# Selective scan with partition = (state, channel of a group of 8), and first-layer attention with maxima

## The chip, the core and the metric

The kernel runs on one core of one Trainium2 chip. The core has a matrix engine (TensorE, PE), a vector engine (VectorE, DVE), an activation engine (ScalarE, ACT), a general engine (GpSimd, POOL) and SyncE (SP), which here only starts transfers. Each works through its own queue in order and waits on semaphores for the others. SBUF is the working memory of 128 partitions, PSUM the small memory that TensorE writes. The metric is the device time of one execution in microseconds (us); before the change it is 20378.7 us, the median of three runs from 20369.83 to 20399.26.

## The reference

The input is 8 images of 64 channels, 64 x 64 pixels (L = 4096 positions), in fp32. Four layers follow each other:

- Layer 0: attention of every position to every position, then a depthwise 3x3 convolution, a 1x1 convolution and a residual.
- Layer 1: a patch norm, then two blocks of 8x8-window attention with 8 heads, each with an MLP.
- Layer 2: a 3x3 filter whose taps depend on position and channel, then a 1x9 convolution.
- Layer 3: a selective scan in four directions over 128 channels with 16 states, then gated output and a multi-scale modulation.

What the change touches is this:

```
# layer 0
scores = einsum('bdn,bdm->bnm', Q, Q) / c ** 0.5        # Q = x, 64 x 4096 per image
prob = softmax(scores, axis=-1)
out = einsum('bnm,bdm->bdn', prob, V)                   # V = relu(bn(w1 x))

# layer 3, for each image, direction k, channel d and state n
h = h * exp(dt_t * A) + dt_t * B_t * u_t                # over 4096 positions t
y_t = sum over n of h * C_t
```

## The kernel before, in words

All is fp32. `tile_kernel` goes through the images in four pairs; the two images of a pair share the 128 partitions, 64 channels each, except in layer 3's scan, which takes one image at a time with its 128 inner channels on the partitions. The whole kernel is unrolled. A scheduler orders each engine's queue from the program and gives out buffers: a pool hands a tile of a tag to the next user when its last user is done, so the number of buffers of a tag sets how far engines run ahead of each other. Five large slabs (one holds 128 x 4356 values) serve X, the padded attention output, values and so on.

**Attention of layer 0** (`layer0_direct`). Both images are worked at once. For each of four column pieces of 1024 and each of 32 row tiles, TensorE makes scores `sd` for image 0 (partitions 0 to 63) and image 1 (64 to 127), each a matmul of 64 rows, so the two use different halves of the array. ScalarE takes the exponential without subtracting a maximum and adds up its rows (`ed`, L508). Then `weigh` (L484) multiplies by the values, one image into PSUM partitions 0 to 63, the other into 64 to 127. At the end the result is multiplied by the reciprocal sums (`prd`). The sums are kept, and at the end of the program `in_range` tests them and a branch would repeat everything with `layer0`, which subtracts maxima; in the runs shown it isn't taken. `block0` is the convolution behind the attention.

**Scan of layer 3** (`ss2d`, `scan_inputs`, `scan`). A unit is a direction `k` and a piece of TC = 1024 positions; an image has 16 units. `scan_inputs` makes B, C (rows `xd`, written to DRAM as `rows`) and the step dt and `dtu` = dt x u, each 128 channels on the partitions. `scan` then loops over the 16 states `n`: SyncE loads B_n and C_n broadcast to all partitions (`bc`, 1 MB, L974), ScalarE makes the decay `da` = exp(dt A_n) (L976), VectorE multiplies dtu by B_n (L978), runs the recurrence (L981) and multiplies by C_n (L985), and TensorE adds the 16 states in PSUM through an identity (`collect`, L969). ScalarE copies the last column as the carry for the next piece (L984). After half the states the next unit's inputs are made (`ahead`).

Lines that the prediction uses beside these: L855 and L860 (`pi`, `pz`: the projection into layer 3, 64 rows), L919 and L935 (`px`, `pd`: B and C, and dt, in `scan_inputs`), L810 and L822 (`pb`, `py`: taps and 1x9 convolution in layer 2), L633 (`kx`: keys times a head mask, on GpSimd, in the window attention), L645 (its scores plus bias, from PSUM), L815 (adding a tap), L319 (squares in a norm, from PSUM), L466 and L471 (`pvd`, values of the attention).

Of the kernel before, what the change touches and what calls it, by code (L numbers as in the profile page):

```python
# [24 lines left out]
TC = 1024  # L25
# [52 lines left out]
def _pack(w):  # L78
# [17 lines left out]
    put("w1T", _dup(f["w1"][:, :, 0, 0].T))  # L96
# [94 lines left out]
class _Net:  # L191
# [39 lines left out]
    def prepare(self):  # L231
# [10 lines left out]
        nc.vector.tensor_tensor(self.w1a[0:64, :], w["w1T"][0:64], sc[0:64, 0, :], ALU.mult)  # L242
        nc.vector.tensor_copy(self.w1a[64:65, :], sc[64:65, 1, :])

        self.w1bd = const.tile([P, P], F32, name="w1bd", tag="w1bd")
        nc.gpsimd.memset(self.w1bd, 0.0)
        for im in range(2):
            lo = slice(64 * im, 64 * im + 64)
            nc.vector.tensor_tensor(self.w1bd[lo, lo], w["w1T"][lo], sc[lo, 0, :], ALU.mult)
        self.b1row = const.tile([1, 8, C], F32, name="b1row", tag="b1row")  # L250
        nc.vector.tensor_copy(self.b1row, sc[0:1, 1, :].unsqueeze(1).to_broadcast([1, 8, C]))
        self.ones = const.tile([P, P], F32, name="ones", tag="ones")
        nc.gpsimd.memset(self.ones, 1.0)
        self.sums = const.tile([P, B // 2, 2, 32], F32, name="sums", tag="sums")
# [30 lines left out]
        self.A = const.tile([P, KDIR, NST], F32, name="A", tag="A")  # L285
        nc.scalar.activation(self.A, w["alog"], AF.Exp)
        nc.vector.tensor_scalar(self.A, self.A, -1.0, None, ALU.mult)
# [51 lines left out]
    def layer0(self, p):  # L339
# [6 lines left out]
        with ExitStack() as st:  # L346
# [78 lines left out]

            self.block0(X, pad, wk, ps, "m")
        return X

    def block0(self, X, pad, wk, ps, tag):

        nc, w = self.nc, self.w
        if True:
            cv = self.flat("cv")
            self.dwconv(cv.rearrange("p (h w) -> p h w", w=64), pad, w["dw2"], None, 64)
            for c in range(NCH):
# [4 lines left out]
                pw = ps.tile([P, CH], F32, name="pw", tag=tag)  # L440
# [4 lines left out]

    def layer0_direct(self, p):

        nc, tc, w = self.nc, self.tc, self.w
        X = self.flat("X")
        nc.sync.dma_start(X, self.x[2 * p : 2 * p + 2].rearrange("b c h w -> (b c) (h w)"))
        pad = self.slab("att").rearrange("p (h w) -> p h w", w=66)
        self.pad_border(pad, 66)
        VT = self.flat("VT").rearrange("p (t c) -> p t c", c=P)
        NB = 1024
        with ExitStack() as st:
            wk = st.enter_context(tc.tile_pool(name="w0d", bufs=2))
            ps = st.enter_context(tc.tile_pool(name="ps0d", bufs=3, space=PSUM))  # L460
            pso = st.enter_context(tc.tile_pool(name="ps0o", bufs=1, space=PSUM))

            for g in range(4):
                pv = ps.tile([P, 8, P], F32, name="pvd", tag="s")
                for h in range(2):
                    nc.tensor.matmul(  # L466
                        pv[:, 4 * h : 4 * h + 4, :], lhsT=self.ones[0:1, :], rhs=self.b1row, start=True, stop=False
                    )
                    for j in range(4 * h, 4 * h + 4):
                        t = 8 * g + j  # L470
                        nc.tensor.matmul(  # L471
                            pv[:, j, :], lhsT=X[:, t * P : (t + 1) * P], rhs=self.w1bd, start=False, stop=(j % 4 == 3)
                        )
                nc.scalar.activation(VT[:, 8 * g : 8 * g + 8, :], pv, AF.Relu)

            parts = wk.tile([P, 2, 32, 4], F32, name="parts", tag="parts", bufs=1)
            half = (slice(0, 64), slice(64, 128))
            for jc in range(L // NB):
                po = pso.tile([P, NB], F32, name="pod", tag="po")

                def weigh(t, es):
                    for h in range(2):
                        for im in range(2):
                            nc.tensor.matmul(  # L484
                                po[half[im], h * CH : (h + 1) * CH],
                                lhsT=VT[:, t, half[im]],
                                rhs=es[im][:, h * CH : (h + 1) * CH],
                                start=(t == 0),
                                stop=(t == 31),
                            )  # L490

                last = None
                for t in range(32):
                    ss = [ps.tile([P, NB], F32, name=f"sd{im}", tag="s") for im in range(2)]
                    for h in range(2):
                        o = jc * NB + h * CH
                        for im in range(2):
                            nc.tensor.matmul(  # L498
                                ss[im][:, h * CH : (h + 1) * CH],
                                lhsT=X[half[im], t * P : (t + 1) * P],  # L500
# [450 lines left out]
    def scan(self, XC, Y, unit, ready, ahead, pools):  # L951
# [20 lines left out]
        for n in range(NST):  # L972
# [14 lines left out]
            if n == NST // 2:  # L987
                following = ahead()
# [107 lines left out]
```

## Time and profile before

| what | value |
|---|---|
| median of three runs | 20378.7 us |
| profiled execution: time / span | 20399.26 us / 20397.1 us |
| instructions in the profile | 109912 |
| busy: PE / DVE / ACT / POOL | 68% / 73% / 31% / 3% |
| mean granted TensorE clock | 0.756 of full |
| one pair of images | 5.1 ms, of which attention 0.53 ms and two scans 1.42 ms each |
| HBM read | 2159.55 MB |

The span is the time from the first to the last instruction. A matmul of 512 fp32 columns appears as two records. "PEclk" is the share of its clock that the throttle granted TensorE: 1.00 or 0.50 at any instant, so a value between is a mixture. In a line of groups stand line, engine, operation, tiles, shape and count, then busy us, mean ns of one, the idle time of the engine before them, and what ended it. The form "64*128 64x512" of a matmul means 64 rows of the array by 128 columns in use, and a moving operand of 64 partitions by 512.

### The profile page before, as it was taken

How to read it: one execution, taken by the hardware profiler on the slowest of the kernel's cores; microseconds unless marked ns; L12 is line 12 of the kernel's file. 1: busy time of each engine (PE TensorE's matmuls, PEld its weight loads, DVE VectorE, ACT ScalarE, POOL GpSimd, SP SyncE). 2: the span in 40 equal slices, each digit the busy share in tenths (PEclk: the TensorE clock that was granted, in tenths of full speed). 3: DMA queues.
4: the chain of work that ended last, by engine and by line, in shares of the span. 5: the costliest groups of instructions: out<-in, count | busy, mean ns of one | idle time of the engine just before them, and what ended most of it. 6: DMA issues, size and time to landing. Idle time of an engine off the chain costs nothing.

```text
span 20397.1 us, 109912 instructions
## 1 busy us (share of the span) xinstructions
PE 13968.1 (68%) x37466; PEld 4708.2 (23%) x37466; DVE 14790.1 (73%) x12346; ACT 6242.7 (31%) x9357; POOL 611.1 (3%) x803
## 2 busy tenths in 40 slices
PE   9787565565978765556597876655659787565665
PEld 3332111111333211111133321111113332111111
DVE  0555998998065599899806559989980656998998
ACT  5331322332533133233253313323325331322332
POOL 0110000000011000000001100000000110000000
PEclk9776776777977677787697767777779776766776
DMA  0000554553000055455300005545530000554553
GB/s 12 1 1 17 196 192 140 197 193 133 4 1 1 21 196 192 143 197 191 130 3 1 1 24 195 192 141 196 192 129 2 1 1 28 195 192 142 197 191 122
DMA packets 569244, 2191.99 MB, mean 107 GB/s; under 512 B 35424, under 2 KB 35424, under 8 KB 568032
## 3 DMA queue, kind: packets, MB, share of 16 engines
q1 hardware_dynamic: 562240, 2164.39, 30.8%
q10 hardware_dynamic: 6432, 20.47, 0.4%
q8 instruction: 298, 4.88, 0.1%
q14 instruction: 274, 2.24, 0.0%
HBM read 2159.55 MB, written 25.17 MB: 107 GB/s over the span
## 4 chain that ended last, share of the span: by engine, by line
DVE 39%; PE 33%; DMA 21%; ACT 4%; issue 2%; DVEq 0%; ACTq 0%; POOL 0%
DMA bc<-rows 21%; DVE h L981 14%; DVE v L978 7%; DVE v L985 7%; PE sd L498 5%; PE pod L484 5%; PE ws L642 4%; DVE n_sd L324 4%; PE av L678 2%; PE n_v L321 2%; PE pb L810 2%; PE pt L670 2%; PE py L822 2%; PE wpv L656 1%; DVE XC L310 1%
## 5 line engine op out<-in xcount | busy, mean ns | idle before, releaser
L969 PE MATMUL y<-v,pack 128*128 128x512 f32 x8192 | 6070.3, 883 | 4309.6 <-DVE v L985 4309.6
L969 PEld LDWEIGHTS y<-v,pack 128*128 128x128 f32 x8192 | 1918.4, 258 | 8488.0 <-DVE v L985 6545.5
L981 DVE TENSOR_TENSOR_SCAN h<-da,carry,v 128x1024 f32<-128x1024 f32 x1536 | 3610.4, 2350 | 142.3 <-DVE v L978 1.4
L976 ACT ACTIVATE da<-dt,A 128x1024 f32<-128x1024 f32 x2048 | 2327.8, 1137 | 1896.1 <-DVE h L981 1894.6
L978 DVE TENSOR_TENSOR v<-dtu,bc 128x1024 f32<-128x1024 f32 x2048 | 2505.5, 1223 | 468.6 <-DMA bc<-rows 448.8
L985 DVE TENSOR_TENSOR v<-h,bc 128x1024 f32<-128x1024 f32 x2048 | 2507.4, 1224 | 61.8
L984 ACT ACTIVATE carry<-h 128x1 f32<-128x1 f32 x1536 | 311.5, 203 | 5571.7 <-DVE h L981 5571.6
L324 DVE RECIPROCAL n_sd<-n_sd 128x512 f32<-128x512 f32 x288 | 963.7, 3349 | 594.4 <-ACT n_sd L323 594.3
L508 ACT ACTIVATE ed<-sd 128x1024 f32<-128x1024 f32 x1024 | 1039.2, 1020 | 866.7 <-PE sd L498 866.5
L981 DVE TENSOR_TENSOR_SCAN h<-da,v 128x1024 f32<-128x1024 f32 x512 | 1173.4, 2292 | 45.7 <-DVE v L978 0.5
L517 DVE COPY att<-pod 128x1024 f32<-128x1024 f32 x16 | 19.6, 1226 | 1578.1 <-PE pod L484 1578.1
L642 PE MATMUL ws<-kx,Q 64*64 64x512 f32 x2048 | 1093.8, 727 | 8.5 <-DVE we L645 6.1
L498 PE MATMUL sd<-X 64*128 64x512 f32 x4096 | 1038.5, 617 | 7.7 <-ACT ed L508 7.7
L484 PE MATMUL pod<-ed,VT 128*64 128x512 f32 x4096 | 998.0, 605 | 0.0
L321 PE MATMUL n_v<-n_sq,pack 128*128 128x512 f32 x576 | 513.2, 988 | 424.0 <-DVE H L332 252.9
L919 PE MATMUL px<-XC,pack 128*36 128x512 f32 x512 | 428.7, 978 | 537.8 <-ACT XC L865 332.3
L633 POOL TENSOR_TENSOR kx<-K,pack 128x512 f32<-128x512 f32 x512 | 536.5, 1052 | 4811.0 <-DVE K L624 2902.9
L678 PE MATMUL av<-wv,et 128*64 128x16 f32 x8192 | 508.4, 221 | 143.6 <-ACT et L672 143.6
L678 PEld LDWEIGHTS av<-wv,et 128*64 128x64 f32 x8192 | 457.5, 150 | 442.3 <-ACT et L672 354.4
L498 PEld LDWEIGHTS sd<-X 64*128 64x128 f32 x4096 | 361.2, 187 | 674.4 <-issue 653.4
L319 ACT ACTIVATE n_sq<-n_c 128x512 f32<-128x512 f32 x288 | 171.9, 597 | 1010.4 <-PE n_c L317 1010.3
L691 ACT ACTIVATE oc<-wot,pack 64x128 f32<-64x128 f32 x512 | 185.7, 363 | 908.9 <-PE wot L687 908.9
(216 smaller groups left out, 12958.1 us busy)
## 6 DMA issues: line engine op xcount, KB each, us to landing
bc<-rows SPq DMA_DIRECT2D x2048, 1024.0 KB, 5.2
rows<-xd ACTq DMA_DIRECT2D x128, 128.0 KB, 2.0
X<-in_x SPq DMA_DIRECT2D x4, 2048.0 KB, 7.9
out<-Y SPq DMA_DIRECT2D x32, 256.0 KB, 2.0
pack<-in_w ACTq DMA_DIRECT2D x1, 3169.0 KB, 16.1
pack<-in_w ACTq DMA_DIRECT2D x1, 424.5 KB, 9.2
```

What stands on the lines that cost most here:

```text
L321: nc.tensor.matmul(pv, lhsT=avg, rhs=sq, start=True, stop=True)
L324: nc.vector.reciprocal(sd, sd)
L484: nc.tensor.matmul(po[half[im], h * CH : (h + 1) * CH], lhsT=VT[:, t, half[im]], rhs=es[im][:, h * CH : (h + 1) * CH], start=(t == 0), sto ...
L498: nc.tensor.matmul(ss[im][:, h * CH : (h + 1) * CH], lhsT=X[half[im], t * P : (t + 1) * P], rhs=X[half[im], o : o + CH], start=True, stop= ...
L508: nc.scalar.activation(e, ss[im], AF.Exp, scale=C**-0.5, accum_out=parts[:, im, t, jc : jc + 1])
L642: nc.tensor.matmul(s[lo], lhsT=Q[lo, cols], rhs=kx[lo], start=True, stop=True)
L678: nc.tensor.matmul(av[lo, hd], lhsT=et[:, j, lo], rhs=v[:, im, hd], start=True, stop=True)
L969: nc.tensor.matmul(y[:, hc], lhsT=w["ident"], rhs=v[:, hc], start=(n == 0), stop=(n == NST - 1))
L976: nc.scalar.activation(da, dt, AF.Exp, scale=self.A[:, k, n : n + 1])
L978: nc.vector.tensor_tensor(v, dtu, bc[:, 0, :], ALU.mult)
L981: nc.vector.tensor_tensor_scan(along(h), along(da), along(v), first, ALU.mult, ALU.add)
L985: nc.vector.tensor_tensor(v, h, bc[:, 1, :], ALU.mult)
```

## The change

Two things change at once.

First, the attention of layer 0 goes back to `layer0`, image by image. For each image TensorE makes all scores once for the row maxima (256 matmuls of 64 rows, `s`, VectorE reduces 1024 at a time), the negative maxima are turned into an extra row of the moving operand, and in a second pass scores of 65 rows are made again (`s`, 256 matmuls), exponentiated, and multiplied by the values (`po`, 256 matmuls of 128 rows: the upper half of the columns holds ones and gives the sums). `layer0_direct`, `in_range` and the branch at the end go.

Second, the scan is laid out anew. A unit is now 512 positions (32 units an image). The partitions of a step are 16 states x 8 channels, and the 16 steps `u` of a unit go over the 16 groups of 8 channels. dt x A is made by TensorE into PSUM (`da`, a matmul whose contraction is one strip of 32 channels, `asel`), ScalarE takes the exponential in place in PSUM. `rows` now holds dtu, and SyncE broadcasts it to the 16 states (`ub`, 1 MB for four steps); B and C are made by TensorE with repeated weights (`BB`, `CC`; C a second time in PSUM as `pc`). GpSimd makes dtu x B for all steps and h x C for the even ones, VectorE makes h x C for the odd ones with C from PSUM, and TensorE sums over states with a selecting matrix into one strip of 32 output partitions (`ysel`, `y`). `v` has four buffers, `h` and `da` three, `y` two.

The diff, cut to its core:

```diff
-TC = 1024
+GD = P // NST
+TC = 512
...
-    put("xpT", np.concatenate([xp[:, RNK:], xp[:, :RNK]], axis=1).transpose(2, 0, 1))
-    dtT = f["dtproj_w"].transpose(2, 0, 1)
-    put("dtT", np.concatenate([np.zeros((2 * NST,) + dtT.shape[1:], np.float32), dtT], axis=0))
+    put("xbT", np.repeat(xp[:, RNK : RNK + NST], GD, axis=1).transpose(2, 0, 1))
+    put("xcT", np.repeat(xp[:, RNK + NST :], GD, axis=1).transpose(2, 0, 1))
+    put("xr", xp[:, :RNK].transpose(1, 0, 2))
+    put("dtT", f["dtproj_w"].transpose(2, 0, 1))
+    e32 = np.eye(32, dtype=np.float32)
+    put("gsel", np.concatenate([e32] * 4, axis=0).reshape(P, 4, GD))
+    put("ysel", np.concatenate([e32.reshape(4, GD, 32)] * NST, axis=1).transpose(1, 0, 2))
     put("dtb", f["dtproj_b"].T)
     put("alog", f["A_logs"].reshape(KDIR, DI, NST).transpose(1, 0, 2))
     put("ds", f["Ds"].reshape(KDIR, DI).T)
...
+        self.asel = const.tile([P, KDIR, 4, NST * GD], F32, name="asel", tag="asel")
+        for k in range(KDIR):
+            for q in range(4):
+                nc.vector.tensor_tensor(
+                    self.asel[:, k, q].rearrange("p (n d) -> p n d", d=GD),
+                    A[:, k, :].unsqueeze(2).to_broadcast([P, NST, GD]),
+                    w["gsel"][:, q, :].unsqueeze(1).to_broadcast([P, NST, GD]),
+                    ALU.mult,
+                )
+        self.xdt = const.tile([P, KDIR, P], F32, name="xdt", tag="xdt")
+        with self.tc.tile_pool(name="psw", bufs=1, space=PSUM) as ps:
+            pw = ps.tile([P, KDIR, P], F32, name="pxdt", tag="pxdt")
+            for k in range(KDIR):
+                nc.tensor.matmul(pw[:, k, :], lhsT=w["xr"][:, k, :], rhs=w["dtT"][:, k, :], start=True, stop=True)
+            nc.scalar.activation(self.xdt, pw, AF.Copy)
         self.dsum = const.tile([P, 1], F32, name="dsum", tag="dsum")
...
-    def layer0_direct(self, p):
...
-    def in_range(self):
...
-        nbc = 2 * NST
-        px = ps.tile([P, TC], F32, name="px", tag="pr")
-        for h in range(TC // CH):
-            nc.tensor.matmul(
-                px[0 : nbc + RNK, h * CH : (h + 1) * CH],
-                lhsT=w["xpT"][:, k, :],
-                rhs=xc[:, h * nr : (h + 1) * nr, :],
-                start=True,
-                stop=True,
-            )
-        xd = wk.tile([nbc + RNK, TC], F32, name="xd", tag="xd", bufs=1)
-        nc.scalar.activation(xd, px[0 : nbc + RNK], AF.Copy)
-        rows = self.dram.tile([nbc, TC], F32, name="rows", tag="rows")
-        nc.scalar.dma_start(rows, xd[0:nbc, :])
-        pd = ps.tile([P, TC], F32, name="pd", tag="pr")
+        BB = wk.tile([P, TC], F32, name="BB", tag="BB")
+        CC = wk.tile([P, TC], F32, name="CC", tag="CC")
+        dt = wk.tile([P, TC], F32, name="dt", tag="dt")
+        dtu = wk.tile([P, TC], F32, name="dtu", tag="dtu")
+        db = w["dtb"][:, k : k + 1]
         for h in range(TC // CH):
             hc = slice(h * CH, (h + 1) * CH)
-            nc.tensor.matmul(
-                pd[:, hc], lhsT=w["dtT"][nbc:, k, :], rhs=xd[nbc:, hc], start=True, stop=True
-            )
-        db = w["dtb"][:, k : k + 1]
-        dtu = wk.tile([P, TC], F32, name="dtu", tag="dtu")
-        nc.scalar.activation(dtu, pd, AF.Abs, bias=db)
-        dt = wk.tile([P, TC], F32, name="dt", tag="dt")
-        nc.vector.tensor_scalar(dt, pd, db, 0.0, ALU.add, ALU.max)
+            pd = ps.tile([P, CH], F32, name="pd", tag="pr", bufs=2)
+            nc.tensor.matmul(pd, lhsT=self.xdt[:, k, :], rhs=xc[:, h * nr : (h + 1) * nr, :], start=True, stop=True)
+            nc.scalar.activation(dtu[:, hc], pd, AF.Abs, bias=db)
+            nc.vector.tensor_scalar(dt[:, hc], pd, db, 0.0, ALU.add, ALU.max)
         nc.scalar.activation(dtu, dtu, AF.Exp, scale=-1.0)
         nc.scalar.activation(dtu, dtu, AF.Ln, bias=1.0)
         nc.vector.tensor_tensor(dt, dt, dtu, ALU.add)
         nc.vector.tensor_tensor(
             dtu.rearrange("p (a b) -> p a b", b=64), dt.rearrange("p (a b) -> p a b", b=64), xc, ALU.mult
         )
-        return rows, dt, dtu
+        rows = self.dram.tile([32, 4, TC], F32, name="rows", tag="rows")
+        nc.scalar.dma_start(rows.rearrange("m r t -> r m t"), dtu)
+        for to, wt in ((BB, "xbT"), (CC, "xcT")):
+            for h in range(TC // CH):
+                pb = ps.tile([P, CH], F32, name="pb3", tag="pr", bufs=2)
+                nc.tensor.matmul(pb, lhsT=w[wt][:, k, :], rhs=xc[:, h * nr : (h + 1) * nr, :], start=True, stop=True)
+                nc.scalar.activation(to[:, h * CH : (h + 1) * CH], pb, AF.Copy)
+        return rows, dt, BB, CC
 
     def scan(self, XC, Y, unit, ready, ahead, pools):
 
         nc, w = self.nc, self.w
         wk, ps = pools
         k, c, at = unit
-        rows, dt, dtu = ready
+        rows, dt, BB, CC = ready
         rev = k >= 2
 
         def along(t):
@@ -961,30 +846,53 @@
 
         if at == 0:
             self.carry = wk.tile([P, NST], F32, name="carry", tag="carry")
-        y = ps.tile([P, TC], F32, name="y", tag="y")
-        def collect(n, v):
+        y = ps.tile([P, TC], F32, name="y", tag="y", bufs=2)
+        pc = ps.tile([P, TC], F32, name="pc3", tag="pc", bufs=1)
+        xc = self.piece(XC, k, c)
+        nr = CH // 64
+        for h in range(TC // CH):
+            nc.tensor.matmul(
+                pc[:, h * CH : (h + 1) * CH],
+                lhsT=w["xcT"][:, k, :],
+                rhs=xc[:, h * nr : (h + 1) * nr, :],
+                start=True,
+                stop=True,
+            )
+        following = None
+        for u in range(NST):
+            q, r = u // 4, u % 4
+            g = 4 * r + q
+            rs = slice(32 * r, 32 * r + 32)
+            if r == 0:
+                ubs = wk.tile([P, 4, TC], F32, name="ub", tag="ub")
+                nc.sync.dma_start(
+                    ubs.rearrange("p r t -> p (r t)"),
+                    rows[GD * q : GD * q + GD].rearrange("d r t -> d (r t)").unsqueeze(0).to_broadcast([NST, GD, 4 * TC]),
+                )
+            ub = ubs[:, r, :]
+            da = ps.tile([P, TC], F32, name="da", tag="da", bufs=3)
             for h in range(TC // CH):
                 hc = slice(h * CH, (h + 1) * CH)
-                nc.tensor.matmul(y[:, hc], lhsT=w["ident"], rhs=v[:, hc], start=(n == 0), stop=(n == NST - 1))
-        following = None
-        for n in range(NST):
-            bc = wk.tile([P, 2, TC], F32, name="bc", tag="bc")
-            nc.sync.dma_start(bc, rows[n :: NST, :].unsqueeze(0).to_broadcast([P, 2, TC]))
-            da = wk.tile([P, TC], F32, name="da", tag="da")
-            nc.scalar.activation(da, dt, AF.Exp, scale=self.A[:, k, n : n + 1])
-            v = wk.tile([P, TC], F32, name="v", tag="v")
-            nc.vector.tensor_tensor(v, dtu, bc[:, 0, :], ALU.mult)
-            h = wk.tile([P, TC], F32, name="h", tag="h")
-            first = 0.0 if at == 0 else self.carry[:, n : n + 1]
-            nc.vector.tensor_tensor_scan(along(h), along(da), along(v), first, ALU.mult, ALU.add)
+                nc.tensor.matmul(da[:, hc], lhsT=self.asel[rs, k, q, :], rhs=dt[rs, hc], start=True, stop=True)
+            nc.scalar.activation(da, da, AF.Exp)
+            v = wk.tile([P, TC], F32, name="v", tag="v", bufs=4)
+            nc.gpsimd.tensor_tensor(v, ub, BB, ALU.mult)
+            h3 = wk.tile([P, TC], F32, name="h", tag="h", bufs=3)
+            first = 0.0 if at == 0 else self.carry[:, g : g + 1]
+            nc.vector.tensor_tensor_scan(along(h3), along(da), along(v), first, ALU.mult, ALU.add)
             if at < NTC - 1:
-                end = h[:, 0:1] if rev else h[:, TC - 1 : TC]
-                nc.scalar.activation(self.carry[:, n : n + 1], end, AF.Copy)
-            nc.vector.tensor_tensor(v, h, bc[:, 1, :], ALU.mult)
-            collect(n, v)
-            if n == NST // 2:
+                end = h3[:, 0:1] if rev else h3[:, TC - 1 : TC]
+                nc.scalar.activation(self.carry[:, g : g + 1], end, AF.Copy)
+            if u % 2:
+                nc.vector.tensor_tensor(v, h3, pc, ALU.mult)
+            else:
+                nc.gpsimd.tensor_tensor(v, h3, CC, ALU.mult)
+            for h in range(TC // CH):
+                hc = slice(h * CH, (h + 1) * CH)
+                nc.tensor.matmul(y[rs, hc], lhsT=w["ysel"][:, q, :], rhs=v[:, hc], start=(q == 0), stop=(q == 3))
+            if u == NST // 2:
                 following = ahead()
 
         yp = y.rearrange("p (a b) -> p a b", b=64)
...
 def tile_kernel(ctx: ExitStack, tc: tile.TileContext, x: bass.AP, packs, layout, out: bass.AP):
     net = _Net(ctx, tc, x, packs, layout, out)
     for p in range(B // 2):
-        t = net.layer0_direct(p)
+        t = net.layer0(p)
         t = net.layer1(t)
         t = net.layer2(t)
         net.layer3(t, p)
-    with tc.If(net.in_range() > 0):
-        for p in range(B // 2):
-            t = net.layer0(p)
-            t = net.layer1(t)
-            t = net.layer2(t)
-            net.layer3(t, p)
 
 
 def kernel(**inputs):
```

The attention that returns, in its inner loops (it stood in the file before and is unchanged):

```
for t in range(32):
    for q in range(4):
        s = ps_s.tile([P, 2, CH], F32, name="s", tag="s")
        for h in range(2):
            o = q * 1024 + h * CH
            nc.tensor.matmul(s[:, h, :], lhsT=X[lo, t * P : (t + 1) * P], rhs=X[lo, o : o + CH], start=True, stop=True)
        nc.vector.tensor_reduce(mx[:, t, q : q + 1], s, AX.XY, ALU.max)
```

More of the change, by code (lines that the diff above doesn't have):

```diff
@@ L241, in prepare @@
         self.w1a = const.tile([65, C], F32, name="w1a", tag="w1a")
-        nc.vector.tensor_tensor(self.w1a[0:64, :], w["w1T"][0:64], sc[0:64, 0, :], ALU.mult)
+        nc.vector.tensor_tensor(self.w1a[0:64, :], w["w1T"], sc[0:64, 0, :], ALU.mult)
         nc.vector.tensor_copy(self.w1a[64:65, :], sc[64:65, 1, :])
[L245 to L254, printed above, removed]
         bn = w["bn23"]
```

115 lines of the change are left out of this document (5 added, 110 removed).

## The prediction

> **What bounds the kernel now.** I read the page's engine shares and its 40 slices first. The four image pairs repeat, VectorE (DVE) fills most slices, and TensorE (PE) alone fills the first slice of each pair.
>
> ```profile
> PE 13968.1 (68%) x37466; PEld 4708.2 (23%) x37466; DVE 14790.1 (73%) x12346; ACT 6242.7 (31%) x9357; POOL 611.1 (3%) x803
> ...
> PE   9787565565978765556597876655659787565665
> ...
> DVE  0555998998065599899806559989980656998998
> ...
> PEclk9776776777977677787697767777779776766776
> ```
>
> Next, the engine table of five stretches of the first pair: attention, the nine taps of layer 2, the input projection of layer 3, and one image's scan.
>
> ```profile
> 50.00:180.00 130.00, 129.25 (x535) 41.98 (x536) 1.23 (x1) 71.02 (x133) 0.00 (x0) 1.00 0.00 1
> 1657.00:1687.60 30.60, 29.93 (x34) 6.61 (x32) 16.72 (x22) 3.70 (x6) 0.00 (x0) 0.50 0.00 0
> ...
> 1917.20:1941.00 23.80, 23.80 (x29) 9.32 (x28) 5.17 (x8) 6.09 (x8) 0.00 (x0) 0.50 0.00 0
> 1983.70:3403.00 1419.30, 846.48 (x1153) 259.06 (x1153) 1301.38 (x832) 422.91 (x545) 0.53 (x4) 0.74 0.55 191
> ```
>
> Columns after the window: its length, then PE, PEld, DVE, ACT, POOL busy, the granted clock, DMA. Attention is PE-bound at clock 1.00. The scan is DVE-bound: 1301 of 1419 us. The two middle rows matter most: PE busy without a gap, yet clock 0.50. The timeline of PE shows which matmuls these are:
>
> ```profile
> 1918.09 1.91 PE L855 MATMUL pi<-H,pack 64*128 64x512 f32 x2
> 1919.79 1.91 PE L860 MATMUL pz<-H,pack 64*128 64x512 f32 x2
> 1921.50 1.91 PE L855 MATMUL pi<-H,pack 64*128 64x512 f32 x2
> ...
> 1992.23 3.63 PE L919 MATMUL px<-XC,pack 128*36 128x512 f32 x4
> 1996.96 1.98 PE L935 MATMUL pd<-xd,pack 4*128 4x512 f32 x4 [1.11 <-ACT xd L927]
> ```
> ```profile
> 305.63 1.99 PE L498 MATMUL sd<-X 64*128 64x512 f32 x8
> 307.55 1.94 PE L484 MATMUL pod<-ed,VT 128*64 128x512 f32 x8
> 309.42 1.13 PE L498 MATMUL sd<-X 64*128 64x512 f32 x4
> ```
>
> A matmul of 512 columns is two records. One with 64 rows starts every 1.707 us for 27 us on end and never gets the full clock; 18-row taps (second stretch) neither. px has all 128 rows and only 36 columns, and after it pd runs four records in 1.98 us: 0.855 us a matmul, 0.43 a record. So rows in use raise the clock, columns don't matter. The flips lie on a grid of 3.4 us: a window 64% full of 128-row work (the first px) did not raise it, one about 80% full (layer 2: py began 2.7 us before the flip) did; windows of about 48% (layer 1's MLP) kept it up, about 40% (start of the second pair) lost it. In the last fence two matmuls on different halves of the array run side by side (8 records in 1.92 us), and each change of tiling costs 0.16 to 0.21 us (1.92 and 1.87 against 4 x 0.427).
>
> The groups of the scan's window give the prices there; the last two lines are from the page:
>
> ```profile
> L981 DVE TENSOR_TENSOR_SCAN h<-da,carry,v 128x1024 f32<-128x1024 f32 x192 | 451.3, 2350 | 18.0 <-DVE v L978 0.5
> L985 DVE TENSOR_TENSOR v<-h,bc 128x1024 f32<-128x1024 f32 x256 | 313.4, 1224 | 7.7
> L978 DVE TENSOR_TENSOR v<-dtu,bc 128x1024 f32<-128x1024 f32 x256 | 313.2, 1223 | 57.1 <-DMA bc<-rows 53.6 <-issue 0.3
> ```
> ```profile
> L633 POOL TENSOR_TENSOR kx<-K,pack 128x512 f32<-128x512 f32 x512 | 536.5, 1052 | 4811.0 <-DVE K L624 2902.9
> L319 ACT ACTIVATE n_sq<-n_c 128x512 f32<-128x512 f32 x288 | 171.9, 597 | 1010.4 <-PE n_c L317 1010.3
> ```
>
> **Part 1, attention.** Removed: 19.7 to 552.8 us in the first pair, 528 in the second; 4 x 530 = 2.12 ms. There each matmul had a partner on the other half of the array. The old pass that returns treats one image after the other, and none of its large matmuls has a partner. Per image, in PE's order:
> - values pv, 32 matmuls of 64 columns, 64 records at 0.25 us (pvd's records at half clock): 16 us, after 8 us for the loads of QK and RQ, which wait for slabs (X takes 7.9 us to land);
> - maxima: 256 scores of 64 rows. The clock starts low, since pv's 65 short rows fill little. So I take the row of pi and pz: 256 x 1.707 = 437 us. The other bound is full clock, 256 x 0.855 = 219. DVE's 128 maxima (1024 from PSUM, near 1.22 us by L985) hide under 3.4 us of PE each;
> - 32 one-column matmuls of the maxima, copies: 20 us;
> - weights and sums: 512 matmuls, alternately two of 65 rows and two of 128. Mean rows 75%, and at half clock one pair lasts 3.42 us, so every second window holds more 128-row work than this: the clock rises, 512 x 0.855 = 438 us plus 4 at the start. Other bound: 876.
>
> Sum 923, times 8 is 7.38 ms: **+5.26 ms**, bounds +3.5 and +8.8. The convolution behind it is the same.
>
> The Trainium skill speaks for the lower bound of the maxima: "TensorE: Matmul & The Clock Gate", section "Why this matters for your kernels", asks only that TensorE be busy for 4 us on end to reach the full clock. By that rule the sum of the whole would be 24.9 ms. The gapless pi and pz at 0.50 contradict it, and I go by them.
>
> **Part 2, scan.** Before: 1419, 1410 and 1416 us in the first, second and last image, 8 x 1415 = 11.32 ms. After: 256 units of 512 positions (32 an image), 16 steps each. Per unit:
> - DVE: 16 scans. 512 elements cost half of 2350 to half plus the 0.14 us that a 1024-element product has beyond two halves (0.681 for L815's 512 against 1.224): 1.18 to 1.31, taken 1.25, as the decay now comes from PSUM and L645 (0.678, PSUM) shows no surcharge. 8 products 5.4, dt, dtu and Y 3.2. Sum 28.7 us.
> - POOL: 24 products at 1.052 (kx): 25.2 us.
> - ACT: 16 exponentials 9.6 (n_sq's 0.597, PSUM), 14 carries of 0.203, five more of 0.6, two table loads of 1.28: 18 us.
> - SP: four loads of 1 MB, half the old bytes, 5.2 us each: hidden.
> - PE: 16 da of 32 rows, 16 y of 128 rows and 32 columns, four full ones. 36 x 0.855 = 30.8 us at full clock, 61.6 at half. The built order alternates: 1.68 changes of tiling a step, 27 x 0.18 = 4.9. Some 8.8 neighbours per unit are two da or two y on different strips; side by side they save about 0.5 each (1.0 at half clock).
>
> So PE becomes the longest. Its queue is in order: y of step u waits for the product, and the da behind it waits too. The order puts da three steps ahead at 57% of the y, two at 32%, one at 11%. The lap da, exp, scan, POOL product, y is 0.86+0.6+1.25+1.05+0.86 and some 0.4 of hand-over, 5 us; with one step ahead PE has only 2.1 us of work for the remaining 4.7, a stall of 2.6, with two about 0.8: 8.7 us a unit (2.9 at half clock). Full clock: 30.8+4.9-4.4+8.7 = 40 us. Half: 61.6+4.9-8.8+2.9 = 60.6.
>
> Which clock? At 40 us, 128-row work is 20 x 0.855 = 17.1 (43%), plus a quarter of the da's 13.7 (8%): 51%, just above where it was lost. At 60.6 it is 56+11 = 67%, just above where it failed to rise. Windows scatter about both, so it flips; with half the time in each the unit takes 1/(0.5/40+0.5/60.6) = 48.2 us, 12.34 ms: **+1.0 ms**, bounds -1.1 (always full) and +6.5 (always half, no neighbours side by side: 69.4).
>
> The waits for bc go (DVE idled 0.45 ms for it, by the page's group of L978), but DVE then waits for PE's da: nothing is won there. The skill's "GPSIMD Engine Reference", section "Engine selection", advises against two-input products on GpSimd, at about twice VectorE's time. The kx row shows 1.5 times; by the page's twice, 24 x 1.36 = 33 us a unit would still lie under PE's, and the sum would be the same.
>
> **Sum.** 20.40 (the profiled execution: span 20397.1 and 2.2 around it, 0.1% above the median of 20378.7) +5.26 +1.0 = **26.7 ms**. Weight products (asel, 16 of about 0.2 us) and the dropped branch at the end are microseconds.
>
> **Rivals.**
> - A: half-filled matmuls get the full clock after all: maxima 219 us, unit 40: 26.7-1.74-2.1 = 22.8 ms. For it: the attention's 1.00; against: pi, pz, taps. 0.13.
> - B: the scan stays at half clock, 65 us a unit (between 60.6 and 69.4): 31.0 ms. For it: 67% is little above the failed 64%. 0.14.
> - C: the second attention pass stays low too, +8 x 438: 30.2 ms. Nothing shows 65 rows mixed with 128. 0.08.
> - D: POOL binds. Were a product 2.2 us with DVE on the same memory, a unit takes 53: 27.9 ms. Against: kx's longest is 1.171. 0.05.
> - E, faster: attention all at full clock (+3.5) and neighbours packed so well that the unit falls to DVE's 28.7 us (-3.97): 19.9 ms. It decides below 30.5 us a unit; PE's 30.8 of matmuls alone speak against it. 0.02.
>
> **How the numbers follow.** The forecast has 0.58 and by itself reaches from 25.0 to 28.9 (unit of 42 to 57 us). The range takes in C, half of B and most of A: 22.9 to 31.2. Slower by over 0.2% (what three runs spread over, 41 us) is all but E: 0.97; 0.01 lies within.
>
> **What would show it.** Attention of a pair near 1.85 ms; clock 0.50 through the maxima, 1.00 after; the scan's clock between 0.6 and 0.85, PE over 85% busy, DVE about 60%, POOL about 55%; DVE's scans waiting for ACT's da and behind it PE. I am wrong if the maxima show 1.00, if a unit is under 42 us, or if POOL's products exceed 1.5 us.

## The result and the profile after

The changed kernel takes 26564.39 us (median of four runs, 26408.26 to 26647.2), the kernel before on the same chip 20383.38 us: ratio 1.302, 95% interval 1.296 to 1.308. It is slower by 6.2 ms. 26.7 ms were forecast. The profiled execution took 26574.03 us, its span is 26572.2.

The engine shares and slices of the changed kernel:

```profile
PE 23680.7 (89%) x50976; PEld 7240.7 (27%) x50976; DVE 13216.0 (50%) x13986; ACT 7024.5 (26%) x13534; POOL 8539.1 (32%) x6961
...
PE   9988799898998879989899887998989988799898
...
PEclk9787666666668766666666886666666687667666
```

TensorE has taken VectorE's place: 89% busy over the whole, 9 or 8 in nearly every slice, and at a clock that is mostly 0.6 or 0.7. GpSimd went from 3% to 32%.

The table by stretches: the first pass (maxima) of the third image, its second pass, and most of one image's scan. Columns after the window are its length, then PE, PEld, DVE, ACT and POOL busy with their instructions, the granted clock, the share of the DMA engines, GB/s.

```profile
6740.00:7150.00 410.00, 408.27 (x568) 162.47 (x567) 132.55 (x109) 15.89 (x19) 0.00 (x0) 0.55 0.00 0
7172.00:7600.00 428.00, 426.87 (x999) 194.25 (x998) 41.95 (x24) 116.98 (x116) 5.31 (x2) 0.96 0.03 5
...
3300.00:4800.00 1500.00, 1389.33 (x2253) 274.64 (x2254) 900.52 (x878) 500.41 (x1157) 975.22 (x763) 0.66 0.41 94
```

In the first pass 64-row scores follow each other without a gap (408 of 410 us) at about half clock; in the second pass the 65-row and 128-row matmuls run at 0.96. In the scan TensorE is 93% busy at clock 0.66, VectorE 60%, GpSimd 65%.

The costliest groups on the page:

```profile
L881 POOL TENSOR_TENSOR v<-ub,BB 128x512 f32<-128x512 f32 x4096 | 5379.1, 1325 | 5385.4 <-PE y L894 3781.0
L884 DVE TENSOR_TENSOR_SCAN h<-da,carry,v 128x512 f32<-128x512 f32 x3584 | 4517.0, 1277 | 3358.1 <-ACT da L879 1551.6
L894 PE MATMUL y<-v,pack 128*32 128x512 f32 x8192 | 4988.0, 879 | 853.4 <-POOL v L891 645.0
L878 PE MATMUL da<-dt,asel 32*128 32x512 f32 x8192 | 4915.7, 915 | 80.6 <-DVE h L884 80.6
L879 ACT ACTIVATE da<-da 128x512 f32<-128x512 f32 x4096 | 2329.7, 581 | 5939.0 <-PE da L878 5911.5
L389 PE MATMUL s<-X 64*128 64x512 f32 x4096 | 3471.2, 1050 | 2.3 <-ACT ge L962 2.3
L891 POOL TENSOR_TENSOR v<-h,CC 128x512 f32<-128x512 f32 x2048 | 2585.8, 1269 | 177.8 <-DVE h L884 177.1
L524 POOL TENSOR_TENSOR kx<-K,pack 128x512 f32<-128x512 f32 x512 | 535.6, 1050 | 6238.1 <-DVE K L515 3246.0
```

VectorE's scans wait first of all for ScalarE's exponentials (1552 of 3358 us), these for TensorE's da (5911 us). TensorE itself waits little: 853 us ahead of y, most of it (645) for GpSimd's h x C product. That product costs 1269 ns; kx, from which I had taken the price, costs 1050.

Where the 6.2 ms are: an image's attention takes 908 us (the first image's second pass ends at 945 us, the next image's values begin there, the first's began at 36), eight make 7.26 ms in place of 2.12. One image's scan takes 1544 us from 3277.8 to 4821.7 and the next 1540, 48.2 us a unit, 12.34 ms in all in place of 11.32.

### The profile page after: what moved, and what is told of

Same layout as the page of the kernel before. It is cut to its first block, busy times and chain, and to the rows that moved or that the text cites. A ratio compares the mean times of both kernels' runs of the same rounds, so it can differ in the third digit from the quotient of the medians.

```text
span 26572.2 us, 151496 instructions
## 1 busy us (share of the span) xinstructions
PE 23680.7 (89%) x50976; PEld 7240.7 (27%) x50976; DVE 13216.0 (50%) x13986; ACT 7024.5 (26%) x13534; POOL 8539.1 (32%) x6961
## 5 line engine op out<-in xcount | busy, mean ns | idle before, releaser
L881 POOL TENSOR_TENSOR v<-ub,BB 128x512 f32<-128x512 f32 x4096 | 5379.1, 1325 | 5385.4 <-PE y L894 3781.0
L884 DVE TENSOR_TENSOR_SCAN h<-da,carry,v 128x512 f32<-128x512 f32 x3584 | 4517.0, 1277 | 3358.1 <-ACT da L879 1551.6
L894 PE MATMUL y<-v,pack 128*32 128x512 f32 x8192 | 4988.0, 879 | 853.4 <-POOL v L891 645.0
L878 PE MATMUL da<-dt,asel 32*128 32x512 f32 x8192 | 4915.7, 915 | 80.6 <-DVE h L884 80.6
L879 ACT ACTIVATE da<-da 128x512 f32<-128x512 f32 x4096 | 2329.7, 581 | 5939.0 <-PE da L878 5911.5
L389 PE MATMUL s<-X 64*128 64x512 f32 x4096 | 3471.2, 1050 | 2.3 <-ACT ge L962 2.3
L891 POOL TENSOR_TENSOR v<-h,CC 128x512 f32<-128x512 f32 x2048 | 2585.8, 1269 | 177.8 <-DVE h L884 177.1
L524 POOL TENSOR_TENSOR kx<-K,pack 128x512 f32<-128x512 f32 x512 | 535.6, 1050 | 6238.1 <-DVE K L515 3246.0
L420 PE MATMUL s<-RQ,QK 65*128 65x512 f32 x4096 | 1923.8, 593 | 0.0
L413 PE MATMUL po<-e,VT 128*128 128x512 f32 x4096 | 1917.9, 592 | 0.0
L889 DVE TENSOR_TENSOR v<-h,pc 128x512 f32<-128x512 f32 x2048 | 1385.0, 676 | 96.7 <-PE pc L855 11.6
```

Of the source, the lines that this page charges most:

```text
L389: nc.tensor.matmul(s[:, h, :], lhsT=X[lo, t * P : (t + 1) * P], rhs=X[lo, o : o + CH], start=True, stop=True)
L413: nc.tensor.matmul(po, lhsT=VT[:, t, :], rhs=e[:, h, :], start=(t == 0), stop=(t == 31))
L420: nc.tensor.matmul(s[:, h, :], lhsT=QK[0:65, t * P : (t + 1) * P], rhs=RQ[0:65, cols], start=True, stop=True)
L878: nc.tensor.matmul(da[:, hc], lhsT=self.asel[rs, k, q, :], rhs=dt[rs, hc], start=True, stop=True)
L879: nc.scalar.activation(da, da, AF.Exp)
L881: nc.gpsimd.tensor_tensor(v, ub, BB, ALU.mult)
```

## The experiments

Each time is the median of four executions (of two for the attention's change alone), measured beside the kernel before on the same chip. That kernel had medians of 20367 to 20382 us there, so chips differ by far less than the changes.

My theory at the start: the rows that a matmul uses set the clock; at 64 rows the first pass stays at 0.50, at 32 rows da holds the scan down, and TensorE at that clock binds both. The rivals: the clock is low for another cause (gaps, what the stage before left); the in-order lap of da, Exp, scan, product and y binds; GpSimd's products bind.

### 1. Each part alone

The scan's change alone (`layer0_direct` and the branch at the end stay):

> The scan's change alone: the attention is that of the kernel before (one pass, both images, its check on the range and the second way kept), the scan is the changed one. If the two parts add up: 26564 - 8 x 908 + 4 x 530 = 21420 us, 1.04 ms above the kernel before, as the unit of 48.2 us says (256 x 48.2 = 12.34 against 8 x 1415 = 11.32 ms). If one part sets the clock or the buffers for the other (rival: the clock that the attention leaves), the scan's unit moves away from 48.2 us and the whole with it, by 256 us for each us.

Measured: 21415.27 us, 1.051 of before (1.050 to 1.053). The order of the scan's instructions on each engine is the changed kernel's.

The attention's change alone:

```
-        t = net.layer0_direct(p)
+        t = net.layer0(p)
...
-    with tc.If(net.in_range() > 0):
-        for p in range(B // 2):
```

> The attention's change alone: the two passes with maxima, one image at a time, with the scan of the kernel before. If the parts add up: 20375 + 8 x 908 - 4 x 530 = 25519 us. If the changed scan costs or saves something in the attention, or the other way round, the sum misses by more than 100 us.

Measured: 25425.78 us, 1.249 of before (1.246 to 1.251). The parts cost 1.04 and 5.06 ms, together 6.10 where the whole change costs 6.18: they add up to within 0.1 ms. Each can be studied by itself.

### 2. All 128 rows in the first pass

```
+                XZ = one.tile([P, L], F32, name="XZ", tag="XZ")
+                nc.gpsimd.memset(XZ[hi, :], 0.0)
+                nc.sync.dma_start(XZ[lo, :], xp[b].rearrange("c h w -> c (h w)"))
...
-    s[:, h, :], lhsT=X[lo, t * P : (t + 1) * P], rhs=X[lo, o : o + CH], start=True, stop=True
+    s[:, h, :], lhsT=XZ[:, t * P : (t + 1) * P], rhs=X[:, o : o + CH], start=True, stop=True
```

> The first pass's score matmuls contract all 128 rows: the stationary operand holds zeros in the other image's 64 rows, the moving one both images. The products are the same and so is their number, 256 an image. If the rows in use set the clock (my theory), the first pass runs at 1.00: 256 x 0.855 = 219 us an image in place of 437, so the whole is 26564 - 8 x 218 = 24820 us, and the second pass and the scan do not change. If the clock stayed low for another reason (the short start of a stage, or what the stage before left), or if the reductions bound the pass (128 x 1.225 = 157 us, so they should not), the pass stays near 437 us and the whole within 0.5% of 26564.

Measured: 24925.81 us (24813.26 to 24995.1), 1.64 ms less; expected were 1.74. The score group of this run, from its page, and two stretches of the third image, in the first and in the second pass:

```profile
L393 PE MATMUL s<-X,XZ 128*128 128x512 f32 x4096 | 1777.0, 597 | 0.0
```
```profile
6320.00:6520.00 200.00, 198.27 (x507) 88.15 (x506) 81.23 (x66) 31.53 (x34) 3.50 (x1) 1.00 0.02 6
6560.00:6960.00 400.00, 398.93 (x962) 181.79 (x961) 71.80 (x51) 96.62 (x96) 5.32 (x2) 0.98 0.03 6
```

The same products with half the rows zero take 597 ns a record in place of 1050, 1777 us in place of 3471, at clock 1.00. TensorE was as busy before. So the rows in use, not the busy time, kept the first pass at half clock.

### 3. All 128 rows for da

```
-                nc.tensor.matmul(da[:, hc], lhsT=self.asel[rs, k, q, :], rhs=dt[rs, hc], start=True, stop=True)
+                nc.tensor.matmul(da[:, hc], lhsT=self.aselz[:, u, :], rhs=dt[:, hc], start=True, stop=True)
```

`aselz` has zeros outside the 32 rows of the step's strip; it is made anew for each direction of an image, 16 small products on VectorE.

> The da matmuls of the scan contract all 128 rows, with a stationary operand per state strip that is zero outside its 32 rows; same sums. Rows theory: the scan's clock goes from 0.66 to 1.00. Then PE's work in a unit is 16 x 0.855 = 13.7 for da, 16 y at about 0.5 side by side = 8, 4 others 3.4 and changes of shape 5, together 30; VectorE's 28.9 (60% of 48.2) lies close. Unit 31 to 40 us, whole 22.2 to 24.5 ms. Rival, the clock is set by PE's gaps and not by rows: da no longer goes side by side with its neighbour, so PE's work grows at 0.66 to about 16 x 1.3 + 12 + 5 + 7 = 45 or more, and the unit is 48 to 55 us, the whole 26.5 to 28.3 ms. Rival, the queue order of da and y (a lap of da, ScalarE's Exp, scan, product, y) binds: no change within 1 us a unit, 26.3 to 26.8 ms, whatever the clock shows.

Measured: 23811.92 us (23791.5 to 23846.6), 1.169 of before; 10.75 us a unit less, 37.4 us. VectorE's order in the scan is the changed kernel's, the other engines' but for about a hundred places of thousands. The da group and the same stretch of the scan, from this run:

```profile
L879 PE MATMUL da<-dt,aselz 128*128 128x512 f32 x8192 | 4247.6, 624 | 78.7 <-DVE h L885 78.7
```
```profile
3300.00:4400.00 1100.00, 1022.36 (x2125) 251.80 (x2126) 871.77 (x862) 484.93 (x1100) 920.90 (x717) 1.00 0.52 121
```

Clock 1.00 throughout, GpSimd 84% and VectorE 79% busy. The rows of da allow the low clock. Whether they alone bring it about is another matter, as experiment 6 shows.

### 4. More buffers

```
-        y = ps.tile([P, TC], F32, name="y", tag="y", bufs=2)
+        y = ps.tile([P, TC], F32, name="y", tag="y", bufs=1)
-            da = ps.tile([P, TC], F32, name="da", tag="da", bufs=3)
+            da = ps.tile([P, TC], F32, name="da", tag="da", bufs=4)
-            v = wk.tile([P, TC], F32, name="v", tag="v", bufs=4)
+            v = wk.tile([P, TC], F32, name="v", tag="v", bufs=6)
-            h3 = wk.tile([P, TC], F32, name="h", tag="h", bufs=3)
+            h3 = wk.tile([P, TC], F32, name="h", tag="h", bufs=4)
```

> The scan gets four da buffers in place of three (y's one bank less pays for it), six v and four h. If the lap of da, Exp, scan, product and y binds a unit (rival), the wait of Exp for da and of GpSimd for y goes, and the unit falls from 48.2 to 40 or less: whole 24.5 ms or less. If PE's rate at its clock binds (my theory: it is 92% busy), at most those 8% can go, and the single y bank adds a wait of some 2 us at each unit's end: unit 45 to 50, whole 25.8 to 27.0 ms.

Measured: 25621.01 us (25564.73 to 25641.81), 44.5 us a unit: below what my theory allowed, far above the rival's 40. The clock in the scan rose to about 0.7, which neither had foreseen, and the scheduler wrote another order. By itself this tells the two apart no better.

### 5. All h x C products on VectorE

```
-            if u % 2:
-                nc.vector.tensor_tensor(v, h3, pc, ALU.mult)
-            else:
-                nc.gpsimd.tensor_tensor(v, h3, CC, ALU.mult)
+            nc.vector.tensor_tensor(v, h3, pc, ALU.mult)
```

> All 16 h x C products of a unit on VectorE, from PSUM at 0.676 us, in place of eight; GpSimd keeps the 16 ub x BB products alone. If TensorE at clock 0.66 binds the scan (my theory now), GpSimd's 62% were not the limit: at most TensorE's waits for those products go, 645 us over the run or 2.5 us of 48.2 a unit, so the whole is 25.9 to 26.7 ms. If GpSimd binds (the rival with products of 1.27 us), a unit falls by up to 8 x 1.27 = 10 us, to 24.0 to 24.5 ms, or until VectorE at 28.9 + 8 x 0.68 = 34 us binds.

Measured: 24711.11 us (24691.4 to 24781.79), 7.2 us a unit less. My theory's 25.9 ms is missed by 1.2 ms; the rival's 24.0 to 24.5 is nearer. But the order on TensorE had changed as well (two da stand in a row at 1288 places in place of 736), so I took a way to shorten GpSimd's products that leaves every queue as it is.

### 6. Shorter products, same order

```
-            nc.gpsimd.tensor_tensor(v, ub, BB, ALU.mult)
+            nc.gpsimd.tensor_tensor(v, ub, BB[:, 0:1].to_broadcast([P, TC]), ALU.mult)
...
-                nc.gpsimd.tensor_tensor(v, h3, CC, ALU.mult)
+                nc.gpsimd.tensor_tensor(v, h3, CC[:, 0:1].to_broadcast([P, TC]), ALU.mult)
```

> The changed kernel with GpSimd's products of the scan cheaper and nothing else: their second operand is one column of BB or CC spread over the 512, as the operands of kx are (1.05 us in place of 1.27 to 1.33), so the scan's values are no longer the reference's. The order of the instructions on every engine is the one of the changed kernel, which it was not in the run with the products on VectorE. If GpSimd's time binds the scan or sits on its chain, 24 x 0.25 = 6 us a unit go: 26564 - 1540 = about 25.0 ms. If TensorE's clock and order bind (my theory: the 1.85 ms of that run came with another order, in which 31 us in 100 were lost to low clock less often), at most the 2.5 us go that TensorE waits for those products: 25.9 to 26.7 ms, the clock still near 0.66 in the scan.

Measured: 24268.95 us (24244.88 to 24296.61), 2.30 ms or 9.0 us a unit less than the changed kernel. From the page of this run, then the scan's stretch:

```profile
L881 POOL TENSOR_TENSOR v<-ub,BB 128x512 f32<-128x512 f32 x4096 | 4438.4, 1095 | 4267.9 <-PE y L894 2705.2
...
L894 PE MATMUL y<-v,pack 128*32 128x512 f32 x8192 | 3998.2, 711 | 720.3 <-POOL v L891 507.2
L878 PE MATMUL da<-dt,asel 32*128 32x512 f32 x8192 | 3958.5, 736 | 89.5 <-DVE h L884 85.9
...
L891 POOL TENSOR_TENSOR v<-h,CC 128x512 f32<-128x512 f32 x2048 | 2117.6, 1039 | 396.4 <-DVE h L884 393.9
```
```profile
3300.00:4300.00 1000.00, 926.58 (x1833) 191.92 (x1832) 713.35 (x715) 414.02 (x944) 648.02 (x614) 0.84 0.49 114
```

GpSimd's time fell by (5379.1 + 2585.8 - 4438.4 - 2117.6) / 256 = 5.5 us a unit, and the unit by 9.0. My theory falls: it gave at most 2.5. The rival falls too, since an engine that binds can't give back more than it saved. TensorE is as busy as before (93%), with the same matmuls in the same order: it was the clock, 0.84 in place of 0.66, and records of y and da that shrank from 879 and 915 to 711 and 736 ns.

The timeline of the changed kernel shows how GpSimd reaches the clock. First GpSimd, then TensorE, in the same microseconds:

```profile
4240.02 3.73 POOL L881 TENSOR_TENSOR v<-ub,BB 128x512 f32<-128x512 f32 x3
4244.10 1.26 POOL L881 TENSOR_TENSOR v<-ub,BB 128x512 f32<-128x512 f32 x1 [0.35 <-PE y L894]
4245.32 1.27 POOL L891 TENSOR_TENSOR v<-h,CC 128x512 f32<-128x512 f32 x1
```
```profile
4238.85 1.12 PE L878 MATMUL da<-dt,asel 32*128 32x512 f32 x2
4239.90 1.25 PE L894 MATMUL y<-v,pack 128*32 128x512 f32 x4
4241.08 1.96 PE L830 MATMUL pb<-XC,pack 128*128 128x512 f32 x2
4242.98 1.05 PE L894 MATMUL y<-v,pack 128*32 128x512 f32 x2
4243.95 1.13 PE L878 MATMUL da<-dt,asel 32*128 32x512 f32 x4
4246.64 1.04 PE L894 MATMUL y<-v,pack 128*32 128x512 f32 x2 [1.56 <-POOL v L891]
4247.62 1.29 PE L878 MATMUL da<-dt,asel 32*128 32x512 f32 x2
4248.84 1.92 PE L894 MATMUL y<-v,pack 128*32 128x512 f32 x2
4250.68 2.08 PE L878 MATMUL da<-dt,asel 32*128 32x512 f32 x4
```

At full clock TensorE outruns GpSimd. The h x C product that the next y needs stands behind four ub x BB products in GpSimd's queue; TensorE waits 1.56 us for it. Two microseconds later every matmul takes twice as long (y 1.92 in place of 1.05, da 2.08 in place of 1.13). At half clock GpSimd mostly keeps up, so little disturbs TensorE; but now the share of 128-row work in a window decides whether the clock returns, and it does so only where several y or full matmuls come together. By the granted-clock records, the 42 low stretches between 3300 and 4800 us last 24 us on the mean. With the shorter products it is 20 stretches of 17 us between 3300 and 4400.

This drop is no single case. The clock's flips lie on a grid of 3.41 us. In that stretch of the changed kernel the clock drops at the end of 41 such windows, and in each of them TensorE idled for 1.0 to 2.0 us ahead of a y: 32 times the wait ended with an h x C product of GpSimd, 9 times with one of VectorE's (L889). Of the 97 windows at full clock that kept it, 5 held more than 1 us of idle time. So VectorE's odd products have a share in it, too, and the shorter products of GpSimd leave it.

### 7. Shorter products at full clock

The same edit on the kernel of experiment 3.

> The same short products of GpSimd on the kernel with da over 128 rows, where the clock is 1.00 with them long (23812 us, unit 37.4); the order on every engine is that kernel's. The scan's values are not the reference's. In the run before, 5.5 us of GpSimd's time a unit gave back 9.0 us. If they worked through the clock (TensorE waits for GpSimd, a wait brings the clock down, and at 0.50 it stays for 20 us; theory now), then here nothing is left to give but TensorE's 2.5 us of waits: 23.1 to 23.8 ms. If GpSimd's own time bounds the unit (rival), 5.5 us or more go again: 22.4 ms or less.

Measured: 23393.88 us (23382.25 to 23416.54), 1.6 us a unit less.

```profile
L895 PE MATMUL y<-v,pack 128*32 128x512 f32 x8192 | 3501.2, 607 | 305.5 <-POOL v L892 231.7
```
```profile
3300.00:4300.00 1000.00, 964.94 (x2024) 240.59 (x2024) 808.72 (x824) 464.45 (x1047) 726.46 (x684) 1.00 0.55 126
```

Where the clock is at 1.00 anyway, the same relief of GpSimd is worth 1.6 us a unit, not 9.0. The difference, 7.4 us by this comparison, went through the clock. So both are needed: da's 32 rows bring the share of full-row work near the edge, and a wait of one or two microseconds for a late product, most often GpSimd's, pushes it over. With all rows of da in use (experiment 3) TensorE also waits ahead of y, 668 us over the run, and keeps the clock.

### 8. The best of both, and what did not help it

The attention of the kernel before with the scan of experiment 3:

> The attention of the kernel before, with the changed scan and its da matmuls over all 128 rows. If the parts add up: 21415 + 23812 - 26564 = 18663 us, below the kernel before by 8%; the scan's unit is 37.4 us, 256 x 37.4 = 9.6 ms against 11.3. If the clock at full speed in the scan needed the changed attention, the unit stays near 48 and the whole near 21.4 ms.

Measured: 18707.76 us (18696.01 to 18740.18), 0.919 of before (0.918 to 0.921). It beats both kernels, and lies 45 us from the sum of the parts. Three attempts to better it:

```
+                yz = self.yselz[:, q, 96 - 32 * r : 224 - 32 * r]
-                nc.tensor.matmul(y[rs, hc], lhsT=w["ysel"][:, q, :], rhs=v[:, hc], start=(q == 0), stop=(q == 3))
+                nc.tensor.matmul(y[:, hc], lhsT=yz, rhs=v[:, hc], start=(u == 0), stop=(u == NST - 1))
```

> As the run before, and the y matmuls write all 128 rows of y (stationary operand zero outside its 32 columns), so that no matmul of the scan changes the shape of the array. The price of 27 changes a unit was estimated at 0.18 us each, 4.9 us. If that is right, the unit falls from 37.4 to between 32 and 35 us (TensorE's floor 36 x 0.855 = 30.8, GpSimd's 24 x 1.31 = 31.4): 17.4 to 18.1 ms. If the changes cost nothing, y loses the neighbours beside it: the unit stays at 37 us or grows by 1 or 2, 18.6 to 19.2 ms.

Measured: 20258.47 us (20247.19 to 20274.16), above both expectations. Two lines of each page, first of the kernel with y in strips, then of this one:

```profile
L1027 PE MATMUL y<-v,pack 128*32 128x512 f32 x8192 | 3578.9, 607 | 672.5 <-POOL v L1024 629.0
L1024 POOL TENSOR_TENSOR v<-h,CC 128x512 f32<-128x512 f32 x2048 | 2605.1, 1279 | 217.6 <-DVE h L1017 217.0
```
```profile
L1031 PE MATMUL y<-v,yselz 128*128 128x512 f32 x8192 | 4463.8, 646 | 1369.2 <-POOL v L1027 1113.6
L1027 POOL TENSOR_TENSOR v<-h,CC 128x512 f32<-128x512 f32 x2048 | 2654.4, 1296 | 2246.6 <-DVE h L1020 2240.3
```

GpSimd now waits ten times as long for h (2240 us for 217), TensorE twice as long for products. The order on all engines was written anew: da stands ahead of y at other places. Which part of the loss is the order's and which the missing neighbours', this run doesn't tell, and what the changes of shape cost stays open.

All h x C products on VectorE (the edit of experiment 5):

> The attention of before, da over 128 rows, and all 16 h x C products on VectorE. The clock is 1.00 in the scan already (18708 us, unit 37.4), so nothing can be won through the clock; GpSimd's 24 x 1.31 = 31.4 us a unit become 21, VectorE's 29.5 become 35. If TensorE's 34 to 35 us with its changes of shape bind, 18.1 to 18.7 ms. If GpSimd bound the unit at 37.4, it falls to VectorE's 35 or TensorE's 34: also 18.1 ms, with TensorE busier than 95%. If VectorE binds with its waits, 18.7 to 19.3 ms.

Measured: 18899.39 us (18863.54 to 18910.1). And with `if u % 4:` in place of `if u % 2:`, so that one in four stays on GpSimd:

> As the run before, with one h x C product in four on GpSimd: GpSimd 20 x 1.31 = 26 us a unit, VectorE 29.5 + 4 x 0.68 = 32. If two engines near their limit cost more than one (lap), this is the fastest, unit 35 to 36, 18.1 to 18.3 ms; if TensorE binds alone, the same as the run before within 1%.

Measured: 19193.03 us (19181.4 to 19203.37). Both are slower than 18708, and what I expected of the second is missed by 0.9 ms. In the scan GpSimd is busy 53% and 65% in place of 83%, TensorE 90% and 91% in place of 94%. So GpSimd's load is not what bounds the unit there: with less of it TensorE idles more. Both kernels had other queue orders again, and how much of the loss is theirs these runs don't tell.

## Why the prediction was right, and where its working was not

The total came out 0.5% above the measurement, and the two parts at +5.26 and +1.0 where +5.06 to +5.15 and +1.04 to +1.14 were measured (each by its own run, or by what the whole has beyond the other).

**The first pass at half clock** (437 us, from pi and pz): 439 us between the values' end at 50 us and the maxima's at 489. The lower bound, by which busy time alone counts, would have needed clock 1.00; experiment 2 reaches it only with 128 rows. The Trainium skill's "TensorE: Matmul & The Clock Gate", section "Why this matters for your kernels", asks for 4 us of busy time alone and, by the prediction's estimate, would have given 24.9 ms; that is what the filled rows measured (24.93), and the unfilled ones, as busy, did not.

**The second pass at full clock** (442): 442 us, 503 to 945. Rival C is out. An image came to 908 and not 923: the 8 us for the loads are not there in the second image, whose values begin at 944.6 as the first's last matmul ends, and the 20 us for the maxima's turn are some 14.

**Rival A**, full clock for half-filled matmuls, fell with the same two stretches. **Rival B**, half clock throughout the scan, fell with its 0.66. **Rival E** would have needed both parts at full clock; even the kernel with all of da's rows takes 37.4 us a unit, above the 30.5 from which E decides.

**The unit of the scan** (48.2 predicted, 48.2 measured) is right in its sum, but sizes in it were off and cancelled:

- The step "with half the time in each". Clock 0.66 means full speed in 0.32 of the time, not 0.5. If the unit at full speed takes 37.4 us (experiment 3; predicted 40), the 0.68 at half speed must do the rest: 100/48.2 - 32/37.4 = 1.22 units in 68 us, 56 us a unit by this estimate, where 60.6 was predicted. The trace agrees: counting the y and da records that start at each clock between 3400 and 4700 us gives 36.5 us a unit at full and 55.7 at half clock. Less time at full clock, a faster unit in both.
- The stalls, "8.7 us a unit (2.9 at half clock)". TensorE's idle time in the same stretch is 6.4 us a unit at full and 1.0 at half clock.
- "POOL: 24 products at 1.052 (kx): 25.2 us". They cost (5379.1 + 2585.8) / 256 = 31.1. kx was the wrong row: its operands are spread over the 512 from fewer values, and experiment 6 finds that price (1.04 to 1.10) for the scan's products when one operand is spread so, too. Here the Trainium skill's "GPSIMD Engine Reference", section "Engine selection", was the nearer guide: about twice VectorE's time, 33 us a unit as an estimate; the product's median of 1266 ns is 1.9 times the 676 of VectorE's.
- VectorE's scan of 512, "1.18 to 1.31". Two products of 512 cost 0.14 us more than one of 1024, not less, so the rows give half of that for each half, 1.18 to 1.24. Measured were 1277 ns; nothing else rests on it.

**Rival D** needed 2.2 us a product and a unit of 53; neither came, and on the mean the products stay under the 1.5 us from which I called myself wrong. But the prediction held GpSimd for hidden under TensorE, and that was the wrong part of the reasoning. I let the clock flip as "windows scatter". They don't scatter by themselves: a wait for a late product makes a window fall short. My remark that with 33 us of products "the sum would be the same" falls with this: from 31.1 to 25.6 us of products the unit moved by 9.0. Had the products cost about the 1.05 us that I assumed, the unit would have taken 39.2 us (experiment 6), and the scan's part would have been -1.3 ms and not +1.0. Two misjudgements, a price too low and a coupling not seen, stood against each other, and the total was right by more luck than the working shows.

**The views** named in advance: attention of a pair 1.82 ms (1.85); TensorE 93% busy in the scan (over 85), VectorE 60% (60), GpSimd 65% (55, low by the same product price); the chain from scan to exponential to da as written.

## What to carry to other kernels

Read the granted clock of each stage beside the rows that its matmuls use: filling a matmul up to 128 rows with zeros took 1.6 ms off one stage here and 2.75 off another. It isn't free where matmuls on different strips run side by side: at full clock two da in a row took 1.13 us with 32 rows and 1.98 with 128. Where TensorE's clock lies near the edge, an engine off the critical path with a third of its time idle is not harmless: one late product cost a 1.56-us wait and then a stretch at half speed, 24 us on the mean. And before a buffer or an engine is changed in a scheduled kernel, compare the queue orders; of the edits of the scan, those that kept the order could be read by themselves; the others moved the time by up to 1.85 ms, and how much of it is the order's I can't say.

## What had not been expected of the hardware

- GpSimd's two-operand product of 512 fp32 took 1266 ns at the median with two full operands (the changed kernel) and 1039 with one spread from a single column (experiment 6).
- VectorE's sums are slower beside a busy GpSimd where both operands lie in SBUF, and its products are not where one lies in PSUM. These groups are from the scan's stretch of the changed kernel, 3300 to 4800 us:

```profile
L889 DVE TENSOR_TENSOR v<-h,pc 128x512 f32<-128x512 f32 x252 | 170.4, 676 | 11.7 <-PE pc L855 1.8
...
L821 DVE TENSOR_TENSOR dt<-dt,dtu 128x512 f32<-128x512 f32 x30 | 36.2, 1207 | 15.9 <-ACT dtu L820 15.9
L822 DVE TENSOR_TENSOR dtu<-dt,XC 128x512 f32<-128x512 f32 x30 | 35.1, 1171 | 0.0
```

  The product with C in PSUM (L889) keeps 676 ns, the sum of two SBUF tiles (L821) takes 1207, where the kernel before, with GpSimd idle, had 681 for such a sum. Over the whole run the 16 sums of L821 that ran with GpSimd idle took 691 to 693 ns, the 235 that GpSimd was busy through took 1259 on the mean. No experiment changed this alone.
- Zeros are as good as data for the clock: the padded matmuls of experiments 2 and 3 hold 1.00 with half and three quarters of their rows zero.
